# A closing product by seven half-size products inside a product that fills TensorE

## The chip, the cores and the metric

One core of one Trainium2 chip runs the whole kernel in one launch. The metric is the device time in microseconds. Before the change it is 1977.8 us, the median of 3 runs (1975.11 to 1980.16). The profiled execution has a span of 1974.9 us and a mean granted TensorE clock of 0.998.

## The reference

Two graph layers on 4096 nodes of 512 features, each with a residual and a layer norm. Layer 0 multiplies the adjacency by a product of signs. Layer 1 is masked attention, weighted by the adjacency:

```python
def _L1_gnn_ref(x, adj, weight, bias, node_w, edge_w):
    node_att = jax.nn.softmax(x @ node_w, axis=0)
    h = x @ edge_w
    e = h @ h.T
    e = jnp.where(adj > 0, e, NEG_BIG)
    edge_att = jax.nn.softmax(e, axis=1)
    combined_att = node_att * edge_att
    support = x @ weight                       # (4096 x 512) @ (512 x 512)
    output = adj * combined_att @ support
    return output + bias

x = _layernorm(x + _L0_gnn_ref(x, adj, L0_gnn_weight), axis=-1)
x = _layernorm(x + _L1_gnn_ref(x, adj, L1_gnn_weight, ...), axis=-1)
```

The kernel computes the last layer as ((adj * attention) @ x1) @ weight. The change concerns the second of these two products, `@ weight`, which is called the closing product here, and the normalization after it.

## The kernel before

The last part of the kernel goes over sixteen blocks (g, r) with g and r from 0 to 3. Block (g, r) multiplies a 1024 x 1024 part of the transposed, weighted attention by rows of x1, by the scheme of seven half-size products instead of eight. Its seven results are added over r into `sums`. Before a block can start, its operand tiles are loaded, shifted by the row maximum (VectorE), put through exp (ScalarE), weighed by the adjacency and combined (VectorE). These steps are spread over the block before, as the queue `first`; what belongs to the previous g is spread in the same way, as the queue `todo`.

```python
def main(self, between):                      # class Aggregate, one block
    ...
    for m in (0, 1, 5, 6, 4, 2, 3) if last else (0, 1, 2, 4, 6, 5, 3):
        rop = (...)[m]()
        lop = lopp.tile([P, BG, HD], F32, name="lop")        # pool of 4 buffers
        nc.sync.dma_start(lop, lop_d[self.r][:, m])
        for h in range(2):
            ps = ps_mm.tile([P, W], F32, name="ps", tag="mm")    # 6 PSUM banks
            for c in range(BG):
                nc.tensor.matmul(ps, lop[:, c, ts(h, P)], rop[:, c, :], ...)      # L887
            if self.r == 0:
                nc.scalar.copy(total[:, m, h, :], ps)
            else:
                nc.vector.tensor_add(total[:, m, h, :], total[:, m, h, :], ps)    # L891
            between()
        ...
        if last:
            for done in self.joins.get(m, ()):
                join(self.g, done, nc.vector)
```

Seven `join` steps (L913) then turn the seven sums into four quarters in place. The closing product follows for each of eight groups of 512 rows (two for each g), with four row blocks each:

```python
class Finish:
    def steps(self):
        yield self.load
        for i in range(BG):
            yield lambda i=i: self.row(i)
        if not self.single:
            yield lambda: self.norm(range(BG))

    def load(self):                           # residuals, four buffers ("rows")
        ...
            nc.gpsimd.dma_start(xb, x1_d[ts(self.A * BG + i, P), :])

    def row(self, i):
        ...
        po = ps_tr.tile([P, D], F32, name="po", tag="tr")        # 2 PSUM banks
        for k in range(KD):                   # KD = 4, D = 512
            nc.tensor.matmul(po, (lower if k // 2 else upper)[:, k % 2, ts(i, P)],
                             w1_s[:, k, :], start=(k == 0), stop=(k == KD - 1))   # L940
        xb = self.xbs[i]
        nc.vector.scalar_tensor_tensor(xb, po, f[:, i : i + 1], xb, ALU.mult, ALU.add)  # L949
        if self.single:
            self.norm([i])

    def norm(self, some_):
        layernorm([self.xbs[i] for i in some_])   # statistics L148, aggregate L149,
        for i in some_:                           # square root L151, scaling L154 (VectorE)
            nc.gpsimd.dma_start(out[ts(self.A * BG + i, P), :], self.xbs[i])      # L956
```

The loop over the blocks, with the two queues, and the end:

```python
    def panel(A):           # row factors of 512 rows; called twice in the block r == 3
        ...
        spread = rows.tile([P, BG, P], F32, name="spread", tag="rows")            # L766
        ... # four transposes of it on TensorE (L769)

    for queue, share in ((first, -(-len(first) // (15 - count[0]))), (todo, count[0] % 2)):
        ...                                   # between(): 14 times in a block
    u.main(between)
    if u.r == HG - 1 and nxt:
        todo.extend(lambda g=u.g, n=n: join(g, n, nc.gpsimd) for n in range(7))
        for half in (1, 0):
            todo.extend(Finish(u.g, half).steps())
for half in (1, 0):
    todo.extend(Finish(HG - 1, half, half == 0).steps())
while todo:
    todo.popleft()()
```

The weight w1 is loaded into the space of `hT`, which the attention product before it reads to its end.

Of the kernel before, what the change touches and what calls it, by code (L numbers as in the profile page):

```python
# [28 lines left out]
def kernel(  # L29
# [13 lines left out]
    nc = tc.nc  # L43
    N, D = x.shape
    NB = N // P
    KD = D // P
# [108 lines left out]

    with (
# [371 lines left out]
    class Rows:  # L528
# [24 lines left out]
        def row(self, i, s, src):  # L553
            b, c = self.r * BG + i, self.c
            if self.i is None:
                e = Uses(1, free_e)
                line, mask = e.buf, self.mask[:, i, :]
            else:
                e = self.a
                line = mask = e.buf.rearrange("p c w -> p (c w)")  # L560
                tc.keep_in_program_order(nc.vector.tensor_scalar(mask, mask, 0.0, NEG_BIG, ALU.is_le, ALU.mult))
            nc.vector.tensor_tensor_reduce(  # L562
                line, mask, src, -1.0, HUGE, ALU.add, ALU.min, accum_out=nmax_c[:, b, c : c + 1]
            )
            s.used()
            if e is not self.a:
                self.a.used()
            masks_h[0] -= self.a.n == 0 or e is self.a

            def exp():  # L570
                nc.scalar.activation(  # L571
                    line, line, AF.Exp, bias=nmax_c[:, b, c : c + 1], scale=-1.0, accum_out=sum_c[:, b, c : c + 1]
                )
                e.used()
                rest[self.r] -= 1

            exps.append((now[0] + 1, exp))
# [322 lines left out]
    def join(g, n, engine):  # L900

        t = sums[:, g % 2]
        m1, m2, m3, m4, m5, m6, m7 = (t[:, m] for m in range(7))
        out_, a, b, op = (
            (m2, m1, m2, ALU.add),
            (m6, m1, m6, ALU.add),
            (m7, m6, m7, ALU.add),
            (m6, m6, m5, ALU.add),
            (m5, m7, m5, ALU.add),
            (m3, m6, m3, ALU.add),  # L910
            (m4, m7, m4, ALU.subtract),
        )[n]
        engine.tensor_tensor(out_, a, b, op)  # L913

    class Finish:


        def __init__(self, g, half, single=False):
            self.g, self.half, self.A, self.single = g, half, g + half * HG, single

        def steps(self):
            yield self.load
            for i in range(BG):
                yield lambda i=i: self.row(i)
            if not self.single:
                yield lambda: self.norm(range(BG))

        def load(self):
            self.xbs = []
            for i in range(BG):  # L930
                xb = rows.tile([P, D], F32, name="xb1", tag="rows")
                nc.gpsimd.dma_start(xb, x1_d[ts(self.A * BG + i, P), :])
                self.xbs.append(xb)

        def row(self, i):
            t = sums[:, self.g % 2]
            upper, lower = (t[:, 2], t[:, 4]) if self.half else (t[:, 1], t[:, 3])
            po = ps_tr.tile([P, D], F32, name="po", tag="tr")
            for k in range(KD):
                nc.tensor.matmul(  # L940
                    po,
                    (lower if k // 2 else upper)[:, k % 2, ts(i, P)],
                    w1_s[:, k, :],
                    start=(k == 0),
                    stop=(k == KD - 1),
                )
            f, _ = panels[self.A]
            xb = self.xbs[i]
            nc.vector.scalar_tensor_tensor(xb, po, f[:, i : i + 1], xb, ALU.mult, ALU.add)  # L949
            if self.single:  # L950
                self.norm([i])

        def norm(self, some_):
            layernorm([self.xbs[i] for i in some_])
            for i in some_:
                nc.gpsimd.dma_start(out[ts(self.A * BG + i, P), :], self.xbs[i])  # L956

    blocks = [Aggregate(g, r) for g in range(HG) for r in range(HG)]
    def couples(B, *As):
# [72 lines left out]
    w1_s = over[:, 2 * 7 * 2 * W :].rearrange("p (k o) -> p k o", o=D)  # L1032
    nc.sync.dma_start(w1_s, w1.rearrange("(k p) o -> p k o", p=P))

    for n, u in enumerate(blocks):
# [12 lines left out]
        count = [0]  # L1048

        def between():  # L1050
            count[0] += 1
            for queue, share in ((first, -(-len(first) // (15 - count[0]))), (todo, count[0] % 2)):
# [9 lines left out]
    for half in (1, 0):  # L1062
        todo.extend(Finish(HG - 1, half, half == 0).steps())
    while todo:
        todo.popleft()()


# [35 lines left out]
```

## Time and profile before

| What | Value |
|---|---|
| Device time, median of 3 | 1977.8 us |
| Span of the profiled execution | 1974.9 us |
| First large product of the sixteen blocks starts | 1080 us |
| Its last one ends | 1933.9 us |
| Last VectorE instruction ends | 1969.4 us |
| VectorE busy, 1272.8 to 1493.4 us (one g) | 168.0 us of 220.6 |
| lop<-lop_d: loads, size, median time to landing | 112, 512 KB, 3.9 us |
| Joins on GpSimd / on VectorE | 21 / 7 |

Times are microseconds from the start of the span, and an instruction's own duration is in nanoseconds. PE is TensorE (PEld its weight loads), DVE is VectorE, ACT is ScalarE, POOL is GpSimd and SP is SyncE; a q behind the name means the queue. L940 is line 940 of the kernel. A group is written as output <- inputs, with partitions x elements and the number of instructions, and behind the bars the busy time, the mean duration, and the idle time of the engine just before such an instruction with what ended it. In the chain, each line has the start, the duration, and what ran or was waited for. An f32 matmul shows as two MATMUL instructions, called passes here.

### The profile page before, as it was taken

To read this page: it belongs to the slowest core of one execution; us is meant where nothing else is said; L and a number is where in the kernel's file an instruction comes from. 1 tells how busy PE (TensorE), PEld (TensorE's weight loads), DVE (VectorE), ACT (ScalarE), POOL (GpSimd) and SP (SyncE) were. 2 spreads that over 40 slices of the span, in tenths; PEclk is the share of its full clock that TensorE was granted. 3 is DMA by queue.
4 is the path that set the end of the run, shared out by engine and by line. 5 is a ranking of instruction groups with operands and counts; after the bars stand their busy time and mean duration, and the time that the engine had idled before them with its cause. 6 is when DMAs were issued, how large, how long until landed. Compare 5 with 4: busy or idle time off the path is not lost.

```text
span 1974.9 us, 18126 instructions
## 1 busy us (share of the span) xinstructions
PE 1954.7 (99%) x6122; PEld 1088.6 (55%) x6122; DVE 1365.8 (69%) x1992; ACT 672.7 (34%) x1107; POOL 402.4 (20%) x507
## 2 busy tenths in 40 slices
PE   9999999999999999999999999999999999999997
PEld 6888888888544455444555444444444444444443
DVE  7767667667764576667466986968678866967634
ACT  5433333333103576666677311121112211131100
POOL 0122222223341111101022111431124121411101
PEclk9999999999999999999999999999999999999999
DMA  8888888887475576677598976775677576675421
GB/s 312 297 322 304 305 320 315 296 327 279 154 266 201 189 284 255 225 258 287 198 365 310 351 270 236 269 253 196 217 264 253 212 252 236 225 288 206 160 60 64
DMA packets 133645, 497.71 MB, mean 252 GB/s; under 512 B 14000, under 2 KB 14000, under 8 KB 125872
## 3 DMA queue, kind: packets, MB, share of 16 engines
q0 software_dynamic: 71488, 262.17, 35.4%
q1 hardware_dynamic: 53712, 205.02, 31.0%
q10 hardware_dynamic: 8352, 29.36, 4.2%
q8 instruction: 48, 0.79, 0.2%
q14 instruction: 45, 0.37, 0.1%
HBM read 376.96 MB, written 119.54 MB: 251 GB/s over the span
## 4 chain that ended last, share of the span: by engine, by line
PE 91%; DMA 3%; issue 2%; DVE 2%; ACT 1%; POOL 1%; POOLq 0%; DVEq 0%; SPq 0%; ACTq 0%
PE ps L887 39%; PE seven L699 12%; PE acc L371 11%; PE acc L370 11%; PE po L940 5%; PE pe L630 4%; PE seven L98 4%; PE pt L600 2%; DMA s_d<-slot 2%; PE acc L243 1%; PE pw L211 1%; PE pt L330 1%; ACT line L571 1%; PE acc L244 1%; DMA more<-in_adj_dram 0%
## 5 line engine op out<-in xcount | busy, mean ns | idle before, releaser
L887 PE MATMUL ps<-lent,lop 128*128 128x512 f32 x960 | 419.3, 592 | 0.0
L370 PE MATMUL acc<-xw,hi 128*128 128x512 f32 x960 | 376.4, 392 | 0.0
L371 PE MATMUL acc<-xw,lo 128*128 128x512 f32 x960 | 374.3, 390 | 0.0
L887 PE MATMUL ps<-slot,lop 128*128 128x512 f32 x832 | 364.0, 592 | 0.0
L887 PEld LDWEIGHTS ps<-lent,lop 128*128 128x128 f32 x960 | 182.0, 190 | 227.2 <-issue 221.0
L887 PEld LDWEIGHTS ps<-slot,lop 128*128 128x128 f32 x832 | 157.8, 190 | 197.8 <-issue 193.2
L362 DVE TENSOR_TENSOR lo<-at,hi 128x1024 fp32r<-128x1024 f32 x120 | 147.0, 1225 | 84.4 <-ACT hi L360 84.3
L371 PEld LDWEIGHTS acc<-xw,lo 128*128 128x128 f32 x960 | 180.3, 188 | 37.1 <-DVE lo L362 0.3
L370 PEld LDWEIGHTS acc<-xw,hi 128*128 128x128 f32 x960 | 180.3, 188 | 36.8
L360 ACT CAST hi<-at 128x1024 fp32r<-128x1024 f32 x120 | 126.4, 1054 | 203.4 <-PE acc L370 148.4
L891 DVE TENSOR_TENSOR over<-over,ps 128x512 f32<-128x512 f32 x168 | 113.6, 680 | 94.0 <-PE ps L887 93.7
L804 ACT ACTIVATE lent<-lent 128x2048 f32<-128x2048 f32 x32 | 61.1, 1910 | 252.4 <-DVE lent L803 239.3
L630 PE MATMUL pe<-hT 128*128 128x512 f32 (+3 forms) x384 | 132.1, 486 | 0.0
L562 DVE CUSTOM_DVE_ANT_0 line<-lent,slot 128x512 f32<-128x512 bf16 x144 | 93.0, 688 | 45.9 <-ACT slot L640 23.0
L571 ACT ACTIVATE line<-line,nmax_c 128x512 f32<-128x512 f32 x160 | 114.8, 724 | 22.2 <-DVE nmax_c L562 22.1
L940 PE MATMUL po<-over 128*128 128x512 f32 x256 | 115.9, 600 | 3.2 <-DVE xb L949 3.2
L803 DVE CUSTOM_DVE_ANT_1 lent<-lent,line 128x2048 f32<-128x2048 f32 x32 | 80.9, 2527 | 49.6 <-DMA lent<-s_d 49.5
L804 ACT ACTIVATE slot<-slot 128x2048 f32<-128x2048 f32 x32 | 61.1, 1910 | 131.2 <-DVE slot L803 120.0
L699 PE MATMUL seven<-hT 128*128 128x512 f32 x192 | 89.8, 593 | 0.0
L630 PEld LDWEIGHTS pe<-hT 128*128 128x128 f32 x384 | 64.6, 191 | 41.4 <-issue 33.8
L940 PEld LDWEIGHTS po<-over 128*128 128x128 f32 x256 | 49.1, 192 | 65.9 <-issue 60.4
L803 DVE CUSTOM_DVE_ANT_1 slot<-slot,line 128x2048 f32<-128x2048 f32 x32 | 75.1, 2353 | 11.4 <-DMA slot<-s_d 10.2
(205 smaller groups left out, 2497.1 us busy)
## 6 DMA issues: line engine op xcount, KB each, us to landing
at<-in_adj_t_dram SPq DMA_DIRECT2D x60, 1024.0 KB, 7.2
lop<-lop_d SPq DMA_DIRECT2D x112, 512.0 KB, 3.9
lent<-in_adj_t_dram POOLq DMA_DIRECT2D x34, 1024.0 KB, 7.2
s_d<-slot POOLq DMA_DIRECT2D x33, 1024.0 KB, 7.0
slot<-s_d POOLq DMA_DIRECT2D x32, 1024.0 KB, 7.7
lent<-s_d POOLq DMA_DIRECT2D x32, 1024.0 KB, 8.3
slot<-in_adj_t_dram POOLq DMA_DIRECT2D x30, 1024.0 KB, 7.4
lent<-in_adj_dram SPq DMA_DIRECT2D x48, 512.0 KB, 5.0
```

Source lines behind the costliest of these rows:

```text
L360: nc.scalar.copy(hi, aq)
L362: nc.vector.tensor_sub(lo, aq, hi.bitcast(F32))
L370: nc.tensor.matmul(acc, hi[:, c, :], xw[:, kb, :], start=(kb == 0), stop=False)
L371: nc.tensor.matmul(acc, lo[:, c, :], xw[:, kb, :], start=False, stop=(kb == NB - 1))
L571: nc.scalar.activation(line, line, AF.Exp, bias=nmax_c[:, b, c : c + 1], scale=-1.0, accum_out=sum_c[:, b, c : c + 1])
L630: nc.tensor.matmul(pe[:, lo * P :], hT[:, k, ts(A * BG + i, P)], hT[:, k, (B * BG + lo) * P : (B + 1) * W], start=(k == 0), stop=(k == KD ...
L699: nc.tensor.matmul(ps, left[m][:, k, q, :], right[m][:, k, :], start=(first and k == 0), stop=(k == KD // 2 - 1), skip_group_check=not first,)
L803: pinned[0](nc.vector._custom_dve(TENSOR_ADD_SAT, out=q, in0=q, in1=m, s0=0.0, s1=-HUGE))
L804: nc.scalar.activation(q, q, AF.Exp)
L887: nc.tensor.matmul(ps, lop[:, c, ts(h, P)], rop[:, c, :], start=(c == 0), stop=(c == BG - 1))
L891: nc.vector.tensor_add(total[:, m, h, :], total[:, m, h, :], ps)
L940: nc.tensor.matmul(po, (lower if k // 2 else upper)[:, k % 2, ts(i, P)], w1_s[:, k, :], start=(k == 0), stop=(k == KD - 1),)
```

## The change

The closing product of two row blocks a and b with w1 (in quarters) is done by the seven-product scheme too: the 512 x 512 weight becomes seven right operands of 256 x 256, three of them combined once, and each pair of row blocks needs four combined left operands. A pair then takes 7 products of two matmuls of 256 columns where it took 8 matmuls of 512. The purpose is fewer columns through TensorE. The results are not combined in PSUM alone: each product is evicted by a multiply-and-add straight into the half of the residual that needs it, or is accumulated on top of a bank that has been evicted already. The order is such that two steps lie between two uses of the bank y.

Beside that:
- The joins of the first three g run on VectorE instead of GpSimd, and the queue `todo` gives one step at each opening instead of at every second one.
- The scaling of the normalization goes to ScalarE, except in the last two groups.
- The last two groups' residuals are loaded during the last block, into large free buffers; both pairs of such a group are interleaved at the end, the half-row statistics are taken as soon as a half is complete, and their outputs are stored by SyncE.
- Layer 0 and all before the blocks keep their instructions and tiles.

The diff, cut to its core:

```diff
+        def steps(self):
+            yield self.load
+            for q in range(2):
+                yield from self.pair(q, ps_tr)
+            yield lambda: self.norm(range(BG))
 
         def load(self):
+            rows_ = x1_d[self.A * W : (self.A + 1) * W, :]
+            if self.last:
+                xb = take()
+                nc.gpsimd.dma_start(xb, rows_.rearrange("(b p) d -> p b d", p=P))
+                self.xbs = [xb[:, i, :] for i in range(BG)]
+                return
...
-        def row(self, i):
-            ...
-            for k in range(KD):
-                nc.tensor.matmul(po, ..., w1_s[:, k, :], start=(k == 0), stop=(k == KD - 1))
...
+        def pair(self, q, pool):
+            ...
+            def combine():
+                s.append(lopp.tile([P, 4, KD // 2, P], F32, name="left1", tag="lop"))
+                s1, s2, s3, s4 = (s[0][:, n] for n in range(4))
+                nc.vector.tensor_add(s1, l21, l22)
+                nc.vector.tensor_sub(s2, s1, l11)
+                nc.vector.tensor_sub(s3, l11, l21)
+                nc.vector.tensor_sub(s4, l12, s2)
+
+            def multiply(name, lop, rop, *to):
+                ...                            # bank x from ps_mm, y and z from ps_tr
+                for k in range(KD // 2):
+                    nc.tensor.matmul(po, lop[:, k, :], w1_r[rop][:, k, :],
+                                     start=(first and k == 0), stop=(k == KD // 2 - 1), ...)
+                for i, h in to:
+                    xb = self.xbs[i][:, ts(h, HD)]
+                    nc.vector.scalar_tensor_tensor(xb, po, f[:, i : i + 1], xb, ALU.mult, ALU.add)
+            ...
+            yield combine
+            yield lambda: multiply("y", l11, 0, (a, 0))
+            yield lambda: (multiply("x", l12, 1, (a, 0)), half_stats(a, 0))
+            yield lambda: multiply("y", 1, 5, (a, 1))
+            yield lambda: multiply("z", 0, 4, (b, 1))
+            yield lambda: (multiply("y", 2, 6, (b, 1)), half_stats(b, 1))
+            yield lambda: (multiply("z", 3, 2, (a, 1)), half_stats(a, 1))
+            yield lambda: (multiply("y", l22, 3, (b, 0)), half_stats(b, 0))
...
+                if self.last:
+                    nc.vector.tensor_scalar(xb, xb, mv[:, k, 0:1], rstd[:, k : k + 1], ALU.subtract, ALU.mult)
+                else:
+                    nc.scalar.activation(xb, xb, AF.Identity, bias=less[:, k : k + 1], scale=rstd[:, k : k + 1])
+                (nc.sync if self.last else nc.gpsimd).dma_start(out[ts(self.A * BG + i, P), :], xb)
...
+        if n == 1:
+            todo.append(lambda: nc.vector.tensor_sub(t3, r22, r12))    # quarters of w1
+            todo.append(lambda: nc.vector.tensor_sub(r12, r12, r11))
+            todo.append(lambda: nc.vector.tensor_sub(t2, r22, r12))
+            todo.append(lambda: nc.vector.tensor_sub(t4, r21, t2))
...
-            for queue, share in ((first, ...), (todo, count[0] % 2)):
+            for queue, share in ((first, ...), (todo, 1)):
...
-            todo.extend(lambda g=u.g, n=n: join(g, n, nc.gpsimd) for n in range(7))
+            todo.extend(lambda g=u.g, n=n: join(g, n, nc.vector) for n in range(7))
...
+        if n == len(blocks) - 2:
+            todo.extend(e.load for e in ends_)
...
+    for e in ends_:
+        for steps in zip(e.pair(0, ps_tr), e.pair(1, ps_mm)):
+            for step in steps:
+                step()
```

More of the change, by code (lines that the diff above doesn't have):

```diff
@@ L913, in join, with __init__ @@
         engine.tensor_tensor(out_, a, b, op)
+    spare = []
     class Finish:
-        def __init__(self, g, half, single=False):
-            self.g, self.half, self.A, self.single = g, half, g + half * HG, single
+        def __init__(self, g, half, last=False):
+            self.g, self.half, self.A, self.last = g, half, g + half * HG, last
+            self.stats = {}
         def steps(self):
             yield self.load
[L923 to L926, printed above, removed]
+            for q in range(2):
+                yield from self.pair(q, ps_tr)
+            yield lambda: self.norm(range(BG))
         def load(self):
+            rows_ = x1_d[self.A * W : (self.A + 1) * W, :]
[4 more added lines that the diff above has]
+                return
             self.xbs = []
@@ L931, in load @@
                 xb = rows.tile([P, D], F32, name="xb1", tag="rows")
-                nc.gpsimd.dma_start(xb, x1_d[ts(self.A * BG + i, P), :])
+                nc.gpsimd.dma_start(xb, rows_[ts(i, P), :])
                 self.xbs.append(xb)
-        def row(self, i):
-            t = sums[:, self.g % 2]
-            upper, lower = (t[:, 2], t[:, 4]) if self.half else (t[:, 1], t[:, 3])
-            po = ps_tr.tile([P, D], F32, name="po", tag="tr")
-            for k in range(KD):
[L940 to L951, printed above, removed]
@@ L953, in norm, with half_stats @@
-        def norm(self, some_):
-            layernorm([self.xbs[i] for i in some_])
-            for i in some_:
-                nc.gpsimd.dma_start(out[ts(self.A * BG + i, P), :], self.xbs[i])
+        def pair(self, q, pool):
+            sums_g = sums[:, self.g % 2]
+            upper, lower = (sums_g[:, 2], sums_g[:, 4]) if self.half else (sums_g[:, 1], sums_g[:, 3])
+            a, b = q, q + 2
+            l11, l12, l21, l22 = (x[:, :, ts(i, P)] for i in (a, b) for x in (upper, lower))
+            tag = "tr" if pool is ps_tr else "mm"
+            bank, s = {}, []
+            def combine():
[6 more added lines that the diff above has]
+            def multiply(name, lop, rop, *to):
+                first = name not in bank
+                if first:
+                    x = name == "x"
+                    bank[name] = (ps_mm if x else pool).tile([P, HD], F32, name="po", tag="mm" if x else tag)
+                po = bank[name]
+                lop = lop if not isinstance(lop, int) else s[0][:, lop]
+                for k in range(KD // 2):
+                    nc.tensor.matmul(
+                        po,
+                        lop[:, k, :],
+                        w1_r[rop][:, k, :],
+                        start=(first and k == 0),
+                        stop=(k == KD // 2 - 1),
+                        skip_group_check=not first,
+                    )
+                f, _ = panels[self.A]
+                for i, h in to:
+                    xb = self.xbs[i][:, ts(h, HD)]
+                    nc.vector.scalar_tensor_tensor(xb, po, f[:, i : i + 1], xb, ALU.mult, ALU.add)
+            def half_stats(i, h):
+                if self.last:
+                    if i not in self.stats:
+                        if not spare:
+                            spare.append(take(free_e))
+                        at = 64 * (self.half * BG + i)
+                        self.stats[i] = spare[0][:, at : at + 12].rearrange("p (h s) -> p h s", h=2)
+                    nc.vector.bn_stats(self.stats[i][:, h, :], self.xbs[i][:, ts(h, HD)])
+                    if h == (0 if i == b else 1):
+                        self.norm([i])
+            yield combine
[6 more added lines that the diff above has]
+            yield lambda: (multiply("y", l22, 3, (b, 0)), half_stats(b, 0))
@@ new lines, in norm @@
+        def norm(self, some_):
+            n = len(some_)
+            mv = small.tile([P, n, nc.vector.BN_AGGR_DIM], F32, name="mv")
+            for k, i in enumerate(some_):
+                if self.last:
+                    nc.vector.bn_aggr(mv[:, k, :], self.stats[i])
+                else:
+                    stats = small.tile([P, nc.vector.BN_STATS_DIM], F32, name="stats")
+                    nc.vector.bn_stats(stats, self.xbs[i])
+                    nc.vector.bn_aggr(mv[:, k, :], stats)
+            both = small.tile([P, 2, n], F32, name="rstd")
+            rstd, less = both[:, 0, :], both[:, 1, :]
+            nc.scalar.activation(rstd, mv[:, :, 1], AF.Sqrt, bias=eps)
+            nc.vector.reciprocal(rstd, rstd)
+            if not self.last:
+                nc.vector.scalar_tensor_tensor(less, mv[:, :, 0], -1.0, rstd, ALU.mult, ALU.mult)
+            for k, i in enumerate(some_):
+                xb = self.xbs[i]
+                if self.last:
+                    nc.vector.tensor_scalar(xb, xb, mv[:, k, 0:1], rstd[:, k : k + 1], ALU.subtract, ALU.mult)
+                else:
+                    nc.scalar.activation(xb, xb, AF.Identity, bias=less[:, k : k + 1], scale=rstd[:, k : k + 1])
+                (nc.sync if self.last else nc.gpsimd).dma_start(out[ts(self.A * BG + i, P), :], xb)
@@ L1033 @@
     nc.sync.dma_start(w1_s, w1.rearrange("(k p) o -> p k o", p=P))
+    r11, r12, r21, r22 = (w1_s[:, k : k + 2, c : c + HD] for k in (0, 2) for c in (0, HD))
+    t2, t3, t4 = (take(free_e).rearrange("p (k o) -> p k o", o=HD) for _ in range(3))
+    w1_r = r11, r21, r22, t4, r12, t2, t3
+    ends_ = [Finish(HG - 1, half, True) for half in (1, 0)]
     for n, u in enumerate(blocks):
@@ L1051, in between @@
             count[0] += 1
-            for queue, share in ((first, -(-len(first) // (15 - count[0]))), (todo, count[0] % 2)):
+            for queue, share in ((first, -(-len(first) // (15 - count[0]))), (todo, 1)):
                 for _ in range(min(share, len(queue))):
@@ L1058 @@
         if u.r == HG - 1 and nxt:
-            todo.extend(lambda g=u.g, n=n: join(g, n, nc.gpsimd) for n in range(7))
+            todo.extend(lambda g=u.g, n=n: join(g, n, nc.vector) for n in range(7))
             for half in (1, 0):
                 todo.extend(Finish(u.g, half).steps())
[L1062 to L1065, printed above, removed]
+        if n == len(blocks) - 2:
+            todo.extend(e.load for e in ends_)
+    assert not todo
+    for e in ends_:
+        for steps in zip(e.pair(0, ps_tr), e.pair(1, ps_mm)):
+            for step in steps:
+                step()
 def kernel(x, adj, L0_gnn_weight, L1_gnn_weight, L1_gnn_bias, L1_gnn_node_w, L1_gnn_edge_w):
```

## The prediction

> **What bounds the kernel now.** I read four views. First the page's busy table and its chain that ended last:
>
> ```profile
> PE 1954.7 (99%) x6122; PEld 1088.6 (55%) x6122; DVE 1365.8 (69%) x1992; ACT 672.7 (34%) x1107; POOL 402.4 (20%) x507
> PE 91%; DMA 3%; issue 2%; DVE 2%; ACT 1%; POOL 1%; POOLq 0%; DVEq 0%; SPq 0%; ACTq 0%
> PE ps L887 39%; PE seven L699 12%; PE acc L371 11%; PE acc L370 11%; PE po L940 5%; PE pe L630 4%; PE seven L98 4%; PE pt L600 2%; DMA s_d<-slot 2%; PE acc L243 1%; PE pw L211 1%; PE pt L330 1%; ACT line L571 1%; PE acc L244 1%; DMA more<-in_adj_dram 0%
> ```
>
> TensorE is 99% busy and is 91% of the chain; the closing product (L940) is 5% of it. Then the chain in order of time, around the first and the last closing products:
>
> ```profile
> 1331.34 3.43 PE po L940 x8
> 1334.78 6.87 PE ps L887 x16
> ...
> 1861.83 72.10 PE ps L887 x168
> 1933.93 13.75 PE po L940 x32
> 1950.82 1.38 POOL out_dram L956 x3
> 1953.61 3.18 DMA xb<-x_d
> 1957.72 8.85 PE po L940 x16
> ```
>
> From 1080.7 to 1933.9 TensorE runs without a gap: only removed matmul time counts there. A full-width pass takes 3.43/8 = 0.429 us (an f32 matmul is two passes). After 1933.9 there is a 3.2 us hole: the last residuals (xb) are loaded into buffers that the preceding output rows still hold. Third, operations grouped with their shapes, and the timeline of a stretch in which 256-wide passes stand in a row (the diagonal blocks have them):
>
> ```profile
> L940 PE MATMUL po<-over 128*128 128x512 f32 x256 | 115.9, 600 | 3.2 <-DVE xb L949 3.2
> 1043.39 0.81 PE L630 MATMUL pe<-hT 128*128 128x256 f32 x3
> ```
>
> Three 256-wide passes of 379 ns span 0.81 us, so they start (0.81-0.379)/2 = 0.216 us apart: half of 0.429, each with a weight load of its own (190 ns) that stays hidden. Fourth, VectorE's and GpSimd's times:
>
> ```profile
> L810 DVE SCALAR_TENSOR_TENSOR lent<-lent,lent x68: 656/684/3636, 1061.0 to 1841.5; 128x512 f32<-128x512 f32 x68
> L913 POOL TENSOR_TENSOR over<-over x21: 2355/2728/6157, 1240.1 to 1728.2; 128x1024 f32<-128x1024 f32 x21
> L913 DVE TENSOR_TENSOR over<-over x7: 1224/1224/1224, 1900.4 to 1934.7; 128x1024 f32<-128x1024 f32 x7
> ```
>
> A weighing (L810) takes 684 ns, but up to 3636 beside a join on GpSimd.
>
> **What the Trainium skill says.** "TensorE: Matmul & The Clock Gate" (Step-by-step: what each phase is for) has weight loads pulled ahead of running matmuls; the trace agrees down to 256 columns. "SBUF — State Buffer" (SBUF: two separate sides) says GpSimd and a VectorE operation with two SBUF inputs exclude each other for a whole instruction. The trace agrees: after 1100 us, 30 L810 and 8 L803 that overlap a GpSimd join average 1601 and 3509 ns, the others 684 and 2287. "Perfetto Trace Analysis" (Optimizing Scalar/DVE Operations) warns of a fixed cost per VectorE instruction, larger from PSUM. It fits: L949 takes 746 ns for 512 columns, against 533 for one column per cycle at the 0.96 GHz that "Trainium Kernel Development and Optimization" (NeuronCore Architecture) gives, so halves cost more than half.
>
> **The change, part by part.**
>
> Matmuls. Before: 8 row groups x 4 blocks x 4 products x 2 passes = 256 passes x 0.429 = 109.9 us. After: 8 x 2 pairs x 7 products x 2 x 2 passes = 448 passes x 0.216 = 96.8 us. Six of the eight groups lie between 1080 and 1934, where TensorE has no gap: 82.4 to 72.5, so -9.9 us straight off the path. The other two lie at the end, where something else takes over (below).
>
> VectorE, for each of the three pairs of groups in the stream. Joins come in at 7 x 1.22 = 8.6 us, but 30 x 0.92 + 8 x 1.22 = 37 us of delay behind GpSimd goes, 12.4 per pair of groups. Evictions: 28 of 256 columns for 8 of 512. I estimate 0.746 - 0.267 = 0.48 us for one (256 columns fewer at 0.96 GHz): 13.4 - 6.0 = +7.4. Operand sums: 16 of 256 columns at 0.42 to 0.49 us (the same shape at L318 to L321), +7. Scaling by ScalarE instead, -8 x 0.55 = -4.4. Sum about +6 us on a period of 220 us, of which VectorE is busy 168 us (1272.8 to 1493.4). The weighed tiles of each later block are ready at least 10 us before TensorE wants them, in steady state 18 or more, so none of this should reach the path.
>
> The end. TensorE needs 112 x 0.216 = 24.2 us, and the 3.2 us hole goes, since the residuals land in big free buffers during the last block. But VectorE, from 1933.97, has: the last accumulation and join 1.9; 28 evictions at 0.40 to 0.48 = 11.2 to 13.4; 7 sums at 0.34 to 0.42 = 2.4 to 2.9 (8 are placed earlier, one more just before); 16 half statistics, estimated 0.69 - 0.27 = 0.42, or 0.35 back to back, = 5.6 to 6.7; 8 each of aggregate, reciprocal and scaling, 0.15 + 0.16 + 0.5 = 6.5. That is 27.6 to 31.4 us, more than TensorE's: **VectorE becomes the bound of the end**. I take 30. It then ends at 1964 where it now ends at 1969.4: -5.4.
>
> After VectorE's last scaling, 5.5 us pass today: the output's DMA is issued by GpSimd at 1969.68, lands at 1972.4, and GpSimd's own drain runs until 1974.1. Issued by SyncE the landing should be the end; I estimate 3.7 us: -1.8.
>
> **What may give back.** The new queue has 7 + 2 x 18 = 43 steps, one for each of 14 openings of a block: 42 fit into three blocks. The 43rd, the second normalization, falls into the fourth block, beside the next panel's spread tile, which takes a residual's buffer. In the changed program's order the panel's transposes stand 18 passes (7.7 us) behind the last closing product. Before them come: eviction, statistics and aggregate (1.8 us), square root and the reciprocal's hops (1.1), one scaling on ScalarE (0.6), output issue (0.5), landing (2.3 to 9.9 us in this trace), the spread (0.6). That is 6.9 to 14.5 us against 7.7. I take a 1.5 us wait, in each of two blocks: **+3**.
>
> Sum: -9.9 - 5.4 - 1.8 + 3 = -14.1 us. 1977.8 - 14 = **1964**.
>
> **Rivals.**
> 1. VectorE falls behind in the stream and TensorE waits for bank or operand. For it: in the fourth block of a group VectorE is busy 45 of 49 us (1444.5 to 1493.4 and 1665 to 1714) and will now wait there for an output DMA, and a 256-wide product needs its bank again two steps (some 8 us) later. Against: the slack above, six rotating banks, and 12 us per pair of groups that come back from GpSimd. It would cost up to 10 us: 1974.
> 2. A late left operand. The sums share four buffers with the streamed tiles (lop), so a load may wait for a product. Followed through the changed program's order, the shortest distance from the freeing product to the first use is 11.6 us of matmul time (20.7 before); these loads landed within 8.5 us after 1130. So no wait; if wrong, 12 pairs x 3 us: the gain is gone.
> 3. The w1 combinations at the start. They stand in VectorE's queue ahead of the last weighing of block 0, while w1 lands only at 1087.9 (8.4 us after its issue, which has to wait for hT's last reader). That delays VectorE's next sums by about 4 us; the first of them has 6.3 us to spare. Probably nothing; if wrong, 1 to 3 us.
> 4. The transposes' wait does not appear and VectorE keeps up at the end (TensorE-bound: about 1961.2 instead of 1964): then 1958.
>
> **Range and chances.** The stream's gain is firm. The uncertain terms are the waits at the panels (0 to 8), the end (2 to 3 either way) and rival 1. That gives 1958 to 1972. Two per cent is 39.6 us; all closing products together are 110 us and the change removes 13 of them, so neither side can be reached without a large surprise: within 2% 0.96.
>
> **What would show it.** Right: 256-wide passes 0.216 us apart; no gap in TensorE from 1080 to the last large product except 1 to 4 us at the panel transposes of the third and fourth group; the last large product ending near 1927; in the last 40 us VectorE nearly gapless, with TensorE waiting for it; no join on GpSimd and no L810 above 0.8 us. Wrong: passes much above 0.216 us, waits of the large products for VectorE or for lop, or an end bound by TensorE.

## The result and the profile after

| | Before | After |
|---|---|---|
| Device time, median | 1978.98 us (1975.11 to 1980.25) | 1956.69 us (1956.30 to 1957.38, 4 runs) |
| Span of the profiled execution | 1974.93 us | 1955.26 us |

The ratio is 0.9891, with a 95% interval of 0.9874 to 0.9908: 1.1% less, some 22 us. The prediction was 1964, and its range ended at 1958; the kernel gained more than expected. By the two profiles, stretch by stretch:

| Stretch | Before, us | After, us | Difference | Predicted |
|---|---|---|---|---|
| all ahead of the blocks (unchanged code) | 1079.55 | 1079.41 | -0.1 | 0 |
| sixteen blocks, first to last large product | 854.38 | 845.27 | -9.1 | -9.9, and +3 at the panels |
| last large product to VectorE's last operation | 35.46 | 27.54 | -7.9 | -5.4 |
| from there to the end of the span | 5.54 | 3.05 | -2.5 | -1.8 |
| sum | 1974.93 | 1955.26 | -19.7 | -14.1 |

The first row is the same program in all the kernels below, and yet it ended between 1076.7 and 1082.3 us from one execution to the next. The spread of the device times has at least this source, so from here on stretches are compared and not spans.

The page of the kernel after, its busy table and the shares of its chain:

```profile
PE 1939.7 (99%) x6314; PEld 1124.2 (57%) x6314; DVE 1385.9 (71%) x2154; ACT 695.1 (36%) x1134; POOL 326.9 (17%) x472
PE 88%; issue 4%; DMA 3%; DVE 3%; ACT 2%; POOL 0%; POOLq 0%; DVEq 0%; ACTq 0%; SPq 0%
```

TensorE is still 99% busy, with 192 more matmul instructions and 15 us less work. GpSimd lost a fifth of its work (402 to 327 us), most of it the joins (67.6 us in the kernel before).

The chain that ended last, in order of time (start, duration, what ran), at the two ends of the blocks:

```profile
1080.55 146.78 PE ps L887 x342
...
1876.61 48.07 PE ps L887 x112
1924.68 19.87 PE po L969 x92
```

The last large product ends at 1924.68 instead of 1933.93, and behind it the closing products run in one piece: the hole of 3.2 us is gone. The end by stages (length; then busy time and number of instructions of PE, PEld, DVE, ACT and POOL; granted clock, DMA share, GB/s):

```profile
1080.00:1924.68 844.68, 844.44 (x2154) 406.39 (x2152) 643.35 (x796) 188.15 (x178) 115.98 (x167) 1.00 0.66 235
1924.68:1948.70 24.02, 24.02 (x112) 20.93 (x111) 22.91 (x66) 1.48 (x5) 0.00 (x0) 1.00 0.12 45
1948.70:1955.30 6.60, 0.15 (x1) 0.00 (x0) 3.40 (x12) 0.89 (x3) 0.00 (x0) 0.87 0.41 159
```

The 112 passes of the end take 24.02 us without a gap (24.2 was worked out), and VectorE was busy 22.91 of those. In the list of waits after 1922 us (engine and line, what it waited for: total, times, longest) TensorE's matmuls wait for nothing; VectorE waits for TensorE instead:

```profile
ACT rstd L1014 <- DVE mv L1007: 67.2, 8, 54.0
PEld ps L887 <- issue: 1.2, 5, 0.2
DVE over L891 <- PE ps L887: 1.2, 1, 1.2
DVE lent L980 <- PE po L969: 0.8, 2, 0.4
```

(ScalarE's long waits for statistics cost nothing.) The groups, by tile, with shortest, median and longest duration in ns and first and last start:

```profile
L810 DVE SCALAR_TENSOR_TENSOR lent<-lent,lent x68: 681/685/694, 1060.9 to 1835.3; 128x512 f32<-128x512 f32 x68
L913 DVE TENSOR_TENSOR over<-over x28: 1218/1220/1226, 1250.5 to 1925.4; 128x1024 f32<-128x1024 f32 x28
L980 DVE SCALAR_TENSOR_TENSOR xb<-po,f,xb x84: 476/479/485, 1309.9 to 1876.7; 128x256 f32<-128x256 f32 x84
```

No weighing (L810) is longer than 694 ns where one took 3636; all 28 joins are on VectorE; an eviction of 256 columns takes 479 ns, as estimated. And the place where a wait of 1 to 4 us was expected, the panel's transposes, in the timeline (start, duration, engine, line; in brackets the idle time before it and what ended it):

```profile
1447.65 0.43 DVE L766 COPY spread<-nm 128x512 f32<-128x512 f32 x1 [2.28 <-DMA out_dram<-xb]
...
1448.35 0.14 PEld L769 LDWEIGHTS ptm<-ident,spread 128*128 128x128 f32 x1 [0.24 <-DVE spread L766]
```

VectorE does wait 2.28 us for the output's transfer before it can write the spread tile; but TensorE, whose turn at the transposes comes at 1448.8, finds it written at 1448.1 (only the weight load waits, 0.24 us).

### The profile page after: what moved, and what is told of

Same layout as the page of the kernel before. It is cut to its first block, busy times and chain, and to the rows that moved or that the text cites. A ratio compares the mean times of both kernels' runs of the same rounds, so it can differ in the third digit from the quotient of the medians.

```text
span 1955.3 us, 18709 instructions
## 1 busy us (share of the span) xinstructions
PE 1939.7 (99%) x6314; PEld 1124.2 (57%) x6314; DVE 1385.9 (71%) x2154; ACT 695.1 (36%) x1134; POOL 326.9 (17%) x472
## 4 chain that ended last, share of the span: by engine, by line
PE 88%; issue 4%; DMA 3%; DVE 3%; ACT 2%; POOL 0%; POOLq 0%; DVEq 0%; ACTq 0%; SPq 0%
PE ps L887 36%; PE seven L699 12%; PE acc L371 11%; PE acc L370 11%; PE pe L630 4%; PE po L969 4%; PE seven L98 4%; PE pt L600 2%; DMA s_d<-slot 2%; PE acc L243 1%; PE pw L211 1%; PE pt L330 1%; ACT line L571 1%; PE acc L244 1%; DMA lent<-in_adj_t_dram 0%
## 5 line engine op out<-in xcount | busy, mean ns | idle before, releaser
L371 PEld LDWEIGHTS acc<-xw,lo 128*128 128x128 f32 x960 | 180.3, 188 | 37.1 <-DVE lo L362 0.3
L370 PEld LDWEIGHTS acc<-xw,hi 128*128 128x128 f32 x960 | 180.3, 188 | 36.8
L803 DVE CUSTOM_DVE_ANT_1 lent<-lent,line 128x2048 f32<-128x2048 f32 x32 | 73.1, 2287 | 24.8 <-DMA lent<-s_d 24.7
L600 PEld LDWEIGHTS pt<-ident,lent 128*128 128x128 f32 x412 | 51.2, 141 | 52.9 <-issue 38.9
L601 ACT COPY slot<-pt 128x512 f32<-128x512 f32 (+3 forms) x126 | 69.6, 555 | 27.0 <-PE pt L600 23.2
```

Source lines behind the costliest of these rows:

```text
L370: nc.tensor.matmul(acc, hi[:, c, :], xw[:, kb, :], start=(kb == 0), stop=False)
L371: nc.tensor.matmul(acc, lo[:, c, :], xw[:, kb, :], start=False, stop=(kb == NB - 1))
L803: pinned[0](nc.vector._custom_dve(TENSOR_ADD_SAT, out=q, in0=q, in1=m, s0=0.0, s1=-HUGE))
```

## The experiments

Thirteen kernels, each the changed kernel with one thing undone, doubled or left out.

### The end: TensorE or VectorE?

**e1** leaves the real statistics of the last two groups out of the end: they are taken from the residuals, long before.

```diff
-                    nc.vector.bn_stats(self.stats[i][:, h, :], self.xbs[i][:, ts(h, HD)])
...
+            todo.extend(lambda e=e, i=i: e.early_stats(i) for e in ends_ for i in range(BG))
```

> The changed kernel, but the 16 half statistics of the last two groups are taken of the loaded residuals during the last block, so 16 x 0.34 = 5.4 us of VectorE work leave the end (the normalization then uses statistics of other values). Theory A, TensorE bounds the end: its 112 passes still run without a gap for 24.0 us, and only the last statistic and a little queueing behind it go, 0.5 to 1 us; last large product to last VectorE instruction 26.5 to 27 us (27.5 in the changed kernel). Theory B, VectorE bounds the end (as predicted): 4 to 5 us less, 22.5 to 23.5.

Measured: the end took 25.75 us instead of 27.54, the device 1955.95 us. VectorE lost 16 operations of 0.34 us, 5.4 us in all, and 1.8 came off the end. If VectorE had been the bound, nearly all would have. But it is more than the 0.5 to 1 of theory A: the last pass still starts 23.8 us after the last large product, so the 1.8 us come out of the 3.5 behind TensorE's passes, where VectorE works off its queue.

**e2** leaves out half of the contraction of the end's closing products: 56 passes instead of 112.

```diff
-                for k in range(KD // 2):
+                K = 1 if self.last else KD // 2
+                for k in range(K):
```

> The changed kernel, but each product of the last two groups leaves out the second half of its contraction: 56 passes instead of 112, 12 us of TensorE time gone from the end, VectorE's work as before. It measures VectorE's own need. Theory A, TensorE bounds the end but VectorE is close behind it: 25 to 26.5 us from the last large product to the last VectorE instruction instead of 27.5, with VectorE gapless. Theory B, VectorE bounds it: 27 to 27.5, no change. A third way, VectorE has much room: 20 or less.

Measured: 26.13 us, 1.4 less, though TensorE had 12 us less to do. Its waits after 1922 us:

```profile
PE po L970 <- DVE left L955: 4.7, 2, 3.5
```

Now TensorE waits for VectorE's sums, and VectorE waits for nothing from 1924.30 to its last operation. So VectorE alone needs 26.1 us and TensorE with what follows its last pass 27.5: they are within 1.4 us of each other, and TensorE is the later one.

**e7** undoes the seven-product scheme in the last two groups only (full-width products with w1, row block after row block, with statistics of whole rows).

```diff
-    for e in ends_:
-        for steps in zip(e.pair(0, ps_tr), e.pair(1, ps_mm)):
-            for step in steps:
-                step()
+    for e in ends_:
+        for i in range(BG):
+            e.row(i)                  # four 512-wide matmuls with w1_s, one eviction
```

> The changed kernel with the last two groups at full width: 64 passes of 0.429 = 27.5 us of TensorE instead of 24.0, early residuals and SyncE stores kept. Theory A, TensorE bounds both: after its last pass eviction, statistics, aggregate, square root, reciprocal, scaling 2.8 us (in the kernel before: 1966.6 to 1969.4); last large product to last VectorE instruction 30.3 instead of 27.5, span +2.8. Theory B, the end by seven is bound by VectorE and gains less or nothing: +1.5 or less.

Measured: the end 30.31 us (+2.8), the last pass starting 26.88 us after the last large product instead of 23.80; the device 1960.18 us, ratio to before 0.9914 (0.9899 to 0.9929). The scheme is worth 2.8 us in these two groups; the rest of what the end gained is not its doing.

**e4** loads the last residuals late again, in the small buffers.

```diff
-            if self.last:
-                xb = take()
-                nc.gpsimd.dma_start(xb, rows_.rearrange("(b p) d -> p b d", p=P))
-                ...
-            todo.extend(e.load for e in ends_)
...
     for e in ends_:
+        e.load()
```

> The changed kernel with the last two groups' residuals loaded into the four rotating row buffers, as before the change; stores still by SyncE. Theory A: the last group's loads wait for the outputs of the one before (normalization 2.5, output 2, load 3.5 us), TensorE stops once y's bank is needed again: a hole of 4 to 6 us, span 1959 to 1961. Rival, the interleaved order hides it: within 1 us of 1955.3.

Measured: the end 33.53 us, +6.0, the largest part of it. The chain of e4:

```profile
1940.84 0.40 POOL xb L936
...
1941.72 4.93 DMA xb<-x_d
...
1946.68 0.50 DVE xb L975
...
1947.22 6.29 PE po L964 x20
```

The load of the residual is issued only when an output row has been scaled, and takes 4.93 us to come. Then twenty passes take 6.29 us where 20 x 0.216 = 4.3 would do: TensorE runs slowly after it has stood still (its granted clock is 0.50 for 3.41 us), which comes back below.

**e3** gives the end's outputs back to GpSimd.

```diff
-                (nc.sync if self.last else nc.gpsimd).dma_start(out[...], xb)
+                nc.gpsimd.dma_start(out[...], xb)
```

> The changed kernel with the last two groups' outputs stored by GpSimd again. Theory A, the end after VectorE's last instruction was GpSimd's drain: 5.5 us again instead of 3.05, span about 1957.7, device time +2.5 us. Rival, the landing alone counts: +0.5 to 0.7 us (2.7 us to land instead of 2.05).

Measured: from VectorE's last operation to the end 5.08 us instead of 3.05, with the end itself unchanged (27.53). The issuing engine is worth 2.0 us. The device time, 1960.3 us, ratio 0.9914 (0.9898 to 0.9931), agrees within its spread.

**v1**, a try at a better kernel, lets ScalarE scale half of the end's rows.

```diff
-            if not self.last:
+            scalar = not self.last or some_[0] < 2
+            if scalar:
...
-                if self.last:
+                if not scalar:
```

> A version meant to beat the changed kernel: in the last two groups the row blocks that are finished first are scaled by ScalarE, which takes two scalings out of VectorE's queue behind the last pass. Theory A, TensorE bounds the end and 3.5 us follow its last pass, 1 us of which is queueing of VectorE's last instructions: 0.5 to 0.9 us less, span about 1954.6. Rival, ScalarE's longer way (one more hop, 0.8 us for a scaling) takes its place: no change or +0.5.

Measured: 27.35 us instead of 27.54; 1957.05 us, ratio 0.989 (0.9874 to 0.9907). Theory A's 0.5 to 0.9 us did not come, and 0.2 can't be told from nothing: the rival of the expectation fits.

### The stream

**e6** undoes the scheme in the first three g and keeps all else, but that the quarters of w1 are combined only in the last block.

```diff
-            for q in range(2):
-                yield from self.pair(q, ps_tr)
+            for i in range(BG):
+                yield lambda i=i: self.row(i)
...
-        if n == 1:
+        if n == len(blocks) - 2:
```

> The changed kernel with the closing products of the six groups inside the stream at full width (4 products of 512 columns per row block), everything else of the change kept, the last two groups by seven. Theory A, the passes are all there is to the stream's part: 24 x 8 x 0.429 = 82.4 instead of 72.5 us, span +9.0 to +9.9, so 1964.3 to 1965.2. Rival, part of the gain is in the other edits of the stream (a new queue share, scaling on ScalarE, joins): +5 or less.

Measured: the blocks took 854.38 us instead of 845.27, without a gap, the three g 220.61, 220.61 and 219.90 as before; 1965.25 us, ratio 0.9941 (0.9924 to 0.9957). The scheme is worth 9.1 us here. Without gaps it would be 9.9: the kernel after has 0.77 us of them. And since the blocks of e6 take exactly what they took before the change, the other edits of the stream (the joins' place, the denser queue, ScalarE's scaling) gain nothing without the scheme.

**e8** does VectorE's operand sums of the stream four times over: 144 more operations.

```diff
-                nc.vector.tensor_add(s1, l21, l22)
-                ...
+                for _ in range(1 if self.last else 4):
+                    nc.vector.tensor_add(s1, l21, l22)
+                    ...
```

> The changed kernel with the four operand sums of each pair inside the stream written four times over (the same values): 12 x 12 more VectorE instructions of 0.34 to 0.42 us, some 55 us in all, 18 per g. It measures how much room VectorE has in the stream. Theory A, room: span within 2 us of 1955.3. Theory B, VectorE is near the bound in the stream: +5 to +20 us, with waits of the closing products for VectorE.

Measured: 1956.55 us. From 1272.8 to 1490.0 VectorE was busy 180.3 us instead of 165.9, and TensorE's only waits in the stream were

```profile
PE po L970 <- DVE xb L981: 0.7, 2, 0.4
```

So 14.4 us of further VectorE work per g cost nothing. VectorE has room, and rival 1 of the prediction is out, in the form in which it was put.

**e9** stores the rows of a group in reverse order, to make the panel's spread tile wait longer.

```diff
-            for k, i in enumerate(some_):
+            todo_ = list(enumerate(some_))
+            for k, i in todo_ if self.last else todo_[::-1]:
```

> The changed kernel, but in the stream the four row blocks of a group are scaled and stored in reverse order, so that the two residual buffers which the next panel's spread tiles take are stored last instead of first (2.1 us later). Theory A, the predicted wait of the panels exists but misses the path by about 1 us (in the changed kernel the spread is ready 6.9 us after the last closing product, the transposes come at 7.7): TensorE waits 1 to 1.5 us in each of the two blocks, span +2 to +3. Rival, the wait is hidden by more than that: no change.

Measured: 1955.11 us and no wait at the panels. But this says less than was hoped: in the trace the spread tile waits for the store that is issued first, in e9 (issued 1441.9, spread written from 1444.6) as in the changed kernel (1444.6 and 1447.65). It takes whichever buffer comes free first, so the reversal only changed which buffer that was. What holds off the wait is told by the changed kernel's own trace, below.

### The joins: where 20 us were hidden

**e5** gives the joins of the first three g back to GpSimd, one word.

```diff
-            todo.extend(lambda g=u.g, n=n: join(g, n, nc.vector) for n in range(7))
+            todo.extend(lambda g=u.g, n=n: join(g, n, nc.gpsimd) for n in range(7))
```

> The changed kernel with the joins of the first three g on GpSimd again. Theory A, VectorE has slack in the stream and the joins' place costs nothing there: span within 1 us of 1955.3, while single weighings (L810) reach 2 to 4 us again and average about 1.6 us beside a join. Theory B, the relief of VectorE is part of the gain: the closing products wait for evictions or for the joins, which on GpSimd take 7 x 2.7 us, at least, before the first left operand; span +2 to +6 us, with waits of TensorE at the start of each group's closing products.

Measured: 1978.26 us (12 runs), ratio to before 1.0009 (0.9999 to 1.0018). The whole gain of the change is gone, far beyond what either theory allowed. The three g took 224.65, 225.34 and 222.55 us. TensorE's waits in the blocks, first of e5:

```profile
PE po L969 <- DVE xb L980: 12.3, 3, 4.5
```

Three holes, one per g, always at a closing product that needs its PSUM bank evicted. The timeline of e5 around the first:

```profile
1318.46 0.48 DVE L980 SCALAR_TENSOR_TENSOR xb<-po,f,xb 128x256 f32<-128x256 f32 x1
1318.99 2.07 PE L969 MATMUL po<-line,left 128*128 128x256 f32 x4 [4.19 <-DVE xb L980]
1320.86 5.57 PE L887 MATMUL ps<-lent,lop 128*128 128x512 f32 x8
```

and the same kinds of work in the changed kernel:

```profile
1324.19 1.03 PE L969 MATMUL po<-line,left 128*128 128x256 f32 x4
...
1325.06 3.60 PE L887 MATMUL ps<-lent,lop 128*128 128x512 f32 x8
```

The hole costs twice. After 4.19 us of standing still the next four passes span 2.07 us instead of 1.03, and eight large ones 5.57 instead of 3.60, with starts 0.853 us apart at first, twice 0.429; the granted clock was 0.50 from 1317.99 to 1324.81. The three holes sum to 12.8 us from start to due start, and the three g lost 20.5: the slow passes are the other 7.7. This is what the Trainium skill, "TensorE: Matmul & The Clock Gate" (What's actually happening) describes: half the clock after an idle window of about 3.4 us, the full one after about as long at work. The trace agrees on the half: the granted clock is 0.50 for 6.82, 6.82 and 3.41 us at the three holes. But in e10 below a hole of 2.72 us already had three slow passes behind it, and one of 3.14 us none. There the measurement differs from the page, and decides.

Why is the eviction late? The evictions stand in VectorE's queue among the weighings of the next block. Some 30 us earlier, in e5:

```profile
1284.70 7.16 POOL L913 TENSOR_TENSOR over<-over 128x1024 f32<-128x1024 f32 x2
1285.20 4.43 DVE L803 CUSTOM_DVE_ANT_1 slot<-slot,line 128x2048 f32<-128x2048 f32 x1
...
1291.61 2.61 DVE L810 SCALAR_TENSOR_TENSOR slot<-slot,slot 128x512 f32<-128x512 f32 x4 [1.98 <-ACT slot L804]
1291.79 0.77 POOL L797 DMA_DIRECT2D slot<-in_adj_t_dram  x1
...
1299.08 1.29 DVE L810 SCALAR_TENSOR_TENSOR lent<-slot,lent 128x512 f32<-128x512 f32 x2 [4.86 <-DMA slot<-in_adj_t_dram]
```

and in the changed kernel:

```profile
1280.27 0.75 POOL L797 DMA_DIRECT2D slot<-in_adj_t_dram  x1 [6.39 <-PE ps L887]
1282.13 2.29 DVE L803 CUSTOM_DVE_ANT_1 slot<-slot,line 128x2048 f32<-128x2048 f32 x1 [1.44 <-DMA slot<-s_d]
1284.34 2.35 DVE L913 TENSOR_TENSOR over<-over 128x1024 f32<-128x1024 f32 x2
...
1288.07 1.30 DVE L810 SCALAR_TENSOR_TENSOR lent<-slot,lent 128x512 f32<-128x512 f32 x2 [1.37 <-DMA slot<-in_adj_t_dram]
```

Two things are seen. The joins on GpSimd stretch VectorE's own operations (4.43 us for a shift of 2.29), as the prediction had it. And GpSimd also issues the loads of the adjacency tiles (L797): with the joins ahead of it in GpSimd's queue, the load goes out at 1291.79 instead of 1280.27, and the weighing that needs it starts at 1299.08 instead of 1288.07, 11 us later. From there to the eviction VectorE works without a pause, as the chain of e5 shows:

```profile
1299.69 1.89 DVE lent L810 x3
1301.58 2.20 DVE lent L819
...
1316.34 2.20 DVE slot L803
1318.54 0.41 DVE xb L980
...
1318.99 2.07 PE po L969 x4
```

The first closing product ended at 1307.07; its eviction starts 11.4 us later, while its bank is wanted again after 7.7 (1314.80). In the changed kernel the same eviction starts 1.8 us after its product (1309.85 after 1308.04). The lateness is also handed on by the buffers, since GpSimd's next load of this kind has to wait until such a weighing frees one:

```profile
POOL slot L797 <- DVE slot L810: 13.3, 1, 13.3
```

The next two kernels ask which of the two counts, and whether more room would hide it; e12 is the control.

**e10**: e5, with five empty steps between the joins and the closing products and four others merged, so that these come four openings (14 us) later.

```diff
+            todo.extend([lambda: None] * 5)
+            todo.append(both(one[0], one[1]))          # load and sums in one step
+            ...
+            todo.append(both(one[17], two[0], two[1])) # normalization, load and sums
```

> Joins on GpSimd as in e5, but five empty steps stand between the joins and the closing products, and four other steps are merged, so that the first closing product of a g comes four openings (about 14 us) later. Theory A (in e5 the joins on GpSimd only make the tiles and VectorE's evictions late, some 9 us, and the denser queue meets that lateness; the kernel before had the room): no hole, 217 us per g, 1957 +-3. Theory B (GpSimd's joins cost TensorE the time wherever the products stand): holes of 4 us with their slow passes remain, about 1978. Something between, say one hole left of three, would say that the second half's products, which keep their place, are met too.

Measured: 1989.47 us, ratio 1.0071 (1.0056 to 1.0086), worse than e5. TensorE's waits for VectorE in the blocks:

```profile
PE po L969 <- DVE xb L980: 18.9, 6, 4.2
```

Six holes. The first of each g is still there, and the timeline shows what the eviction stands behind:

```profile
1328.98 2.50 DVE L810 SCALAR_TENSOR_TENSOR slot<-slot,slot 128x512 f32<-128x512 f32 x4 [7.79 <-DMA slot<-in_adj_t_dram]
...
1331.92 2.29 DVE L803 CUSTOM_DVE_ANT_1 lent<-lent,line 128x2048 f32<-128x2048 f32 x1 [0.45 <-DMA lent<-s_d]
1334.13 0.48 DVE L980 SCALAR_TENSOR_TENSOR xb<-po,f,xb 128x256 f32<-128x256 f32 x1
...
1334.66 1.22 PE L969 MATMUL po<-line,left 128*128 128x256 f32 x2 [3.59 <-DVE xb L980]
```

Theory A, that 14 us of distance would do, fell: the weighing before it waits 7.79 us for the next late load, and starts at 1328.98 where the changed kernel has it at 1318.98 (of these 10 us, 1.6 are a later start of the blocks). The lateness fades only slowly: with the later start taken off it is 11.8 us at the weighing of 1301.48 and still 8.4 at this one, since each load waits for a buffer that an earlier weighing frees (GpSimd waited 13.5 us for this one, until 1319.28). The other three holes (2.5 to 2.8 us) are of this experiment's own making: with the normalization and the next residuals' load in one step, an eviction waits 4.5 us for a residual whose buffer has just been stored.

**e11**: e5, with these loads issued by SyncE instead of GpSimd.

```diff
-            nc.gpsimd.dma_start(self.q[n], s_d[...])
+            nc.sync.dma_start(self.q[n], s_d[...])
...
-            nc.gpsimd.dma_start(a, adj_t[...])
+            nc.sync.dma_start(a, adj_t[...])
```

> Joins on GpSimd as in e5, but the loads of the attention and adjacency tiles (L790, L797), which in e5 stand behind the joins in GpSimd's queue, are issued by SyncE. Theory A (of the 10.8 us by which VectorE's left sums are late in e5, about 5.8 come from the load that GpSimd issues 11.5 us late): VectorE no longer waits for that load, the lateness shrinks to 5 us, the hole of 4.35 us goes or is below 1, about 1958 to 1962. Theory B (the delay of VectorE's own operations beside the joins is what counts): hole and slow passes stay, 1974 to 1980.

Measured: 1965.84 us, ratio 0.9953 (0.9938 to 0.9967), some 11 us better than e5 by the two ratios. TensorE's waits in the blocks:

```profile
PE ps L887 <- DMA lop<-lop_d: 5.5, 4, 2.5
PE po L969 <- DVE xb L980: 4.4, 3, 1.9
```

The result lies between the ranges of the two theories. The waits for evictions fell from 12.3 us to 4.4 with the joins still on GpSimd. New is a wait for the left operands, whose loads now share SyncE's queue with the others.

**e12**, the control: the changed kernel, joins on VectorE, with the loads on SyncE.

```diff
-            nc.gpsimd.dma_start(self.q[n], s_d[...])
+            nc.sync.dma_start(self.q[n], s_d[...])
...
-            nc.gpsimd.dma_start(a, adj_t[...])
+            nc.sync.dma_start(a, adj_t[...])
```

> Control: the changed kernel (joins on VectorE) with only the issue of these loads moved to SyncE. Both theories: no hole in the stream, 217 us per g, 1957 +-2. If SyncE's queue makes loads late by itself (its own loads of left operands wait in order), gaps appear here too and e11 has to be read against this run.

Measured: 1954.17 us, ratio 0.9896 (0.9880 to 0.9913), the blocks 844.97 us with 0.47 us of gaps. The loads' queue alone changes nothing that can be seen. So the waits of e11 come from the joins on GpSimd, whether by VectorE's delay or by late buffers. Of the 12.3 us of waits for evictions in e5, up to 8 came through the loads that stood behind the joins (up to, since a wait for a left operand also gives VectorE time to catch up); 4.4 are left with the loads out of the way. How far those 4.4, and the waits for left operands, come from the stretched VectorE operations alone was not separated.

## Why the prediction was wrong, by its own steps

**The stream's matmuls, -9.9: right.** Measured -9.1, and e6 gives 9.1 for the scheme alone. The 256-wide passes start 0.216 us apart, as read off the diagonal blocks. The missing 0.8 us are small gaps.

**The panels, +3: wrong, measured 0.** The step that failed is "I take a 1.5 us wait, in each of two blocks". The chain was put at 6.9 to 14.5 us against 7.7; in the trace the last closing product ends at 1441.21 and the spread tile is written at 1448.08, 6.87 us, the short end of the range. The term that set the range was the output's landing, "2.3 to 9.9 us in this trace". In the kernel before, the long landings stand at just this place: the stores ahead of the two panels took 5.8 to 6.1 and 8.6 to 9.9 us, and VectorE waited for them before it could write the spread tiles (waits of the kernel before):

```profile
DVE spread L766 <- DMA out_dram<-xb: 9.9, 2, 6.5
```

In the kernel after, the stores at this place land in 2.7 to 3.0 us, and the two waits sum to 4.5. So the mis-sized term is the landing, and TensorE is spared by 0.7 us only (1448.08 against 1448.77): with a landing of 5.8 us, by this sum, it would have waited some 2 us. Why the landings became short was not tried. What the traces show beside it: before, these stores were issued 1.3 and 0.8 us after a 1 MB load in GpSimd's queue (1425.61 after 1424.34, 1646.59 after 1645.76), after, 4.0 us (1444.61 after 1440.64, 1662.19 after 1658.22). I had carried a duration over to a new order without asking what made it long.

**The end, -5.4: too small, measured -7.9.** The failed step is "VectorE becomes the bound of the end. I take 30". TensorE stays the bound, as rival 4 had it (rival 4, with no wait at the panels either, said 1958, and both of its halves came true): its 24.0 us of passes plus 3.5 us of eviction, statistics and scaling behind the last one make 27.5. VectorE was busy 22.91 + 3.40 = 26.3 us, below the 27.6 to 31.4 worked out, and e2 gives 26.1 for VectorE alone. The terms were right at their lower ends: evictions about 0.40 us back to back, half statistics about 0.34. One was oversized: aggregate, reciprocal and scaling, put at 0.81 us per row block, take 0.12 + 0.07 + 0.45 = 0.64 in the chain of the changed kernel, 1.4 us in eight:

```profile
1947.65 0.12 DVE mv L1007
...
1948.51 0.07 DVE rstd L1015
...
1948.98 0.45 DVE lent L1021
```

Back to back, the next operation starts before the last has quite ended (evictions of 0.48 us start 0.40 apart, scalings of 0.53 to 0.55 us are followed after 0.45); with so many short ones, I should have used the shorter figure throughout. Within the end the early residuals are worth 6.0 us (e4) and the half-size products 2.8 (e7). They overlap, so they don't add up. Beside the 3.2 us hole that the prediction named, the slow passes behind it went too: in the kernel before, the last sixteen passes take 8.85 us where 6.87 would do (the prediction shows the line and does not read it). Hole and slow passes are 5.2 us, and e7, which has neither hole nor scheme, ends 5.15 us below the kernel before (30.31 against 35.46).

**After VectorE's last operation, -1.8: right in kind, sized too small.** 3.05 us instead of 3.7; e3 shows 2.0 us for SyncE against GpSimd; the other 0.5 is not accounted for.

**"So none of this should reach the path": true of the changed kernel, and wrongly reasoned.** I counted the joins' move as VectorE time, per g 8.6 us in and 12.4 us of delay out, on an engine with slack, so worth nothing. e8 confirms the slack: 14 us more per g cost nothing. And e5 shows that moving the joins is worth the 20 us of stream that would otherwise be lost. Both hold because slack in busy time is not what counted, but when one eviction is done, behind weighings that GpSimd's joins made late. The kernel before had the late loads too: its weighings at the same places start at 1300.2 instead of 1288.1 and at 1325.1 instead of 1319.0. Yet its TensorE had no gap. Its first closing product comes after these weighings (1331.18 to 1334.78), its eviction follows at 1342.51, 7.7 us later, and the bank is wanted again only after 17.0 us (1351.78), where e5 wants it after 7.7. That this room is what saved the kernel before is argued, not tried: no run has the half-size products in its slower queue. The prediction saw that delay in the L810 rows, and not that GpSimd's joins stood ahead of loads.

**The sum.** The panels 3.0, the end 2.5, the last part 0.7, less 0.8 in the stream: 5.4 of the 5.6 us between -14.1 and -19.7. The rest between 1964 and 1956.7, some 2 us, lies within the spread of the unchanged first part.

## What to carry to other kernels

Before you call work on a slack engine free, ask what stands behind it in that engine's queue: an engine that both computes and issues loads makes late loads of its computations, and where a later load needs a buffer that the late work frees, the lateness is handed on (here it fell from 11.8 only to 8.4 us in 27). Ask how long a bank may wait for its eviction, too, when products become smaller and follow each other faster. When you carry a duration over to a new order, ask what made it as long as it is. Count chains of short operations by the distance of their starts. And where two engines end within a microsecond or two, give both versions their full chain up to the last instruction before saying which one is the bound.

## What the runs showed of the hardware

- A hole in TensorE can cost more than itself. In e5 holes of 12.8 us in sum cost 20.5: at each, the granted clock was 0.50 for 6.82, 6.82 and 3.41 us, with 512-wide passes 0.853 us apart instead of 0.429.
- The length of a hole does not decide alone. Holes of 2.51 us (e11) and 2.52, 2.72 and 2.80 us (e10) had slow passes behind them; one of 3.14 us (e10) and two of 1.81 and 1.91 us (e11) had none. In e10 the half clock sets in at 1333.34, 1405.02, 1630.30, 1790.73 and 1858.99, all of them multiples of 3.413 us apart. The hole of 3.14 us, 1560.09 to 1563.22, has a point of this grid in its midst (1562.03). So where a hole lies on the grid seems to count; what share of a period has to be idle is not shown.
- The engine that issues the last store matters: 5.08 us from VectorE's last operation to the end with GpSimd, 3.05 with SyncE.
